# Layer 1 of a two-layer cross-attention: even entries with their image tokens first, one group of value products for two mixed tiles, M and the semantic probabilities sent with 80 rows

## The chip, the core and the metric

The kernel runs on one core of one Trainium2 chip, in one launch. The metric is device time in microseconds: the median of three runs. Beside it stands one profiled execution, from which all durations below are read.

## What is computed

Two cross-attention layers, one after the other, over 16 batch entries ("entries") of 256 query tokens with 320 channels, 20 heads of 16. The context has 256 tokens of 512 features for each entry. Layer 1 (the functions whose names end in 0) is the part that the change touches:

```python
text = encoder_hidden_states[:, :77]          # 77 text tokens
ip = encoder_hidden_states[:, 77:]            # 179 image tokens
q = hidden_states @ Wq
k_text, v_text = text @ Wk, text @ Wv
ip_k, ip_v = ip @ Wk_ip, ip @ Wv_ip
text_out = softmax(q_h k_text_h * scale) v_text_h              # for each head
text_probs = softmax((q @ k_text.T) * scale)                   # over all heads at once
q_sem = text_probs @ text
sem = (q_sem @ ip.T) * scale                                   # the same for every head
ip_probs = softmax(q_h ip_k_h * scale + 0.5 * sem) * spatial_mask
out = (text_out + ip_probs ip_v_h) @ Wout + bout + hidden_states
```

The softmax over the 77 text tokens and the one over the 179 image tokens are separate; both are taken in one tile of 256 keys. Layer 2 has the same shape with 252 text and 4 image tokens, and is unchanged.

## The kernel before

All operands are kept as a rounded high part and a low part, so a product over 512 features is a group of 12 matmuls (4 blocks of 128 features, three terms each; `prod`).

**Slots.** One slot is one group of 4 heads of one entry. Layer 1 takes slots 0 to 79 (entry b has slots 5b to 5b+4), layer 2 slots 80 to 159. Two entries, 2c and 2c+1, make a pair c and take ten slots, 10c to 10c+9. In slot k TensorE makes the scores of slot k+2 (`score0`, L737, in the PSUM tile S, of which there is one; VectorE takes their maxima, L738 text and L739 image, and so frees S), the maxima turned round (`maxima0`, L745, then an ACT copy to `mt` and four small DMAs from ACT's queue into the rows of `qs`), the transposed scores of slot k in two halves t = 0 and 1 (`turned0`, L761, PSUM tiles T), their exponentials on ACT (L764), a product with the semantic weights `rs` on GpSimd, POOL in the profile (L767), and at the next slot's first fifth the products with the values (`attend0`, `values0`, L794), 24 matmuls of 32 columns.

**Fillers.** Between these steps stand the tasks that prepare later entries. Each has a list of times in slots, and `fill` steps those that are due, so TensorE's order is fixed by these numbers; TensorE is the only engine of the main loop whose order is written, the other queues (ACT, DVE, POOL, SP) are put in order by the scheduler of the framework, each then running in its order. Tasks: `k0` (`keys0`: context of a pair loaded by `context`, split into high and low parts by `in_turn`/`halves`, L163 on ACT and L166 on POOL or DVE; then the keys), `q0` (`queries0`, with the split of x: ACT L281, POOL or DVE L282, DVE L283), `m0t` (`tokens0`: M, the products of an entry's text and image tokens), `v0` (`values0_`: the values), `s0` (`semantic0`: text probabilities turned round in `tph`; L663 on DVE reads a PSUM bank and frees it), `c0` (output product). The X banks of PSUM, three, are shared by all fillers in turn.

**Layout of an entry.** The 256 keys are text first (0 to 76), then image (77 to 255). With tiles of 128 keys, tile 0 is mixed (77 text, 51 image) and tile 1 is image alone. So `values0_` makes three groups of 12 products of 128x320 for each entry: text values of tile 0, image values of tile 0, image values of tile 1; ACT copies each to the value tile `vr` (L418), with masks `tmask` for the two of tile 0. The column of ones that gives the softmax sums is set once (`marks`). In L794 value group `vt` = 0 and 1 read P of t = 0, and `vt` = 2 reads t = 1.

**Semantic scores and maxima.** The stacks `ks` and `qs`, four of each, have 48 rows of keys or queries, from row 48 (`XROW`) 77 rows of M or of the text probabilities, and from row 125 two rows that subtract the maxima of text and of image. `stacks0` fills them by DMA from SP's queue: `ks<-kd` and `qs<-qd` (48 rows), `qs<-tph` (77 rows x 4 heads x 256) and `ks<-M` (77 x 4 x 179, the image columns alone; the text columns are zero from the start, and the two last rows of `ks` are set once by `fields`). Groups g = 0 to 3 of an entry send M and the probabilities; g = 4 finds them in its stack.

Of the kernel before, what the change touches and what calls it, by code (L numbers as in the profile page):

```python
# [26 lines left out]
T1 = S - NIP  # L27
DUP = S // 2 - NIP
# [21 lines left out]
def xattn2(  # L50
# [60 lines left out]
    words, slots = {"ctb": 1024, "cta": 1024, "raw": 512, "rawc": 512, "both": 2 * (S - T0), "kb": 936, "si": 256, "sp": 128, "wC": 2 * 4 * (H * D + NIP), "mt": S, "mx": 2, "tmp": (NG + 1) * 48, "kst": 4 * S, "rs": 2 * S, "P": 4 * S}, {}  # L111
# [77 lines left out]
    def in_turn(parts, wait, tag="raw", eng=nc.vector, later=False):  # L189

        ahead, parts, tags = [], list(parts), tag.split()
        for i in range(len(parts) + 1):
# [6 lines left out]
            for j in new:  # L199
                src, hi, lo = parts[j]  # L200
                raw = buf(tags[j // 2 % len(tags)], [128, 512], bufs=2)
                shape = src.shape
                raw = raw[:, : shape[1]] if len(shape) == 2 else raw.rearrange("p (k n) -> p k n", k=shape[1])
                (queued if later else lambda inst: inst)(dma(raw, src))
                ahead.append((hi, lo, raw))
# [55 lines left out]

    def context(b, n, wait=0):

        tiles, parts = [], []
        for k in range(0, 4, 3 - n):
            src = cT_d[:, b * S : (b + n) * S].rearrange("(k p) t -> p k t", p=128)[:, k : k + 3 - n]
            ct = buf("cta" if n == 1 or k < 2 else "ctb", [128, 2, 512], FR, bufs=SIZES["CTA" if n == 1 or k < 2 else "CTB"], name="ct")
            split = lambda t: t.rearrange("p (k t) -> p k t", t=n * S)
            parts.append((src, split(ct[:, 0]), split(ct[:, 1])))
            tiles.append(ct)  # L270
        yield from in_turn(parts, wait, "rawc raw" if b == 2 and n == 2 else "rawc", nc.gpsimd if wait and b != 2 else nc.vector, n == 2 and b > 2)
        if n == 2:
            return lambda s, k: tiles[k][:, s].rearrange("p (b t) -> p b t", b=2)
# [12 lines left out]
    ct = [buf(t, [128, 2, 512], FR, bufs=2, name="ct") for t in ("cta", "cta", "ctb", "ctb")]  # L286
    ct0 = {0: lambda s, k, tiles=ct: tiles[k][:, s].rearrange("p (b t) -> p b t", b=2)}
# [27 lines left out]
    hsn = const_tile([128, 3, 8, 2, 16], "hsn")  # L315

    def constants():
# [3 lines left out]
        for i in range(SIZES["NR"]):  # L321
            nc.gpsimd.memset(f(ks[i]), 0.0)
# [10 lines left out]

    def fields():

        ind0 = buf("nt", [128, 2, 8, 32], bufs=2, name="ind0").rearrange("p a f c -> p (a f c)")[:2, :S]
        dma(ind0, ind0_d)
        yield
        ind0r = buf("mt", [8, S], FR, name="ind0r")[:2]
        nc.scalar.copy(ind0r, ind0)  # L340
        yield
        for i in range(SIZES["NR"]):
            dma(ks[i][XROW + T0 : KS0], ind0r.unsqueeze(1).to_broadcast([2, 4, S]))
        yield
# [15 lines left out]
    def keys0(c):  # L360
# [8 lines left out]
        for m in range(3):  # L369
            kst = buf("kst", [128, 2, 2, S], FR, bufs=SIZES["KST"])  # L370
            for w, lo, hi, a, z in ((wk0, 0, T0 + 1, 0, T0), (wki0, T0 - 1, S, T0, S)):
                kp = bank()[:, : 2 * (hi - lo)].rearrange("p (b t) -> p b t", b=2)
                prod_m(kp, w, m, lambda s, k: ct(s, k)[:, :, lo:hi], 4)
                n = 64 if m == 2 else 128
                evacuate(kst[:, 0, :, a:z], kst[:, 1, :, a:z], kp[:, :, a - lo : z - lo], m)
                if a:
                    keys_out(kd[0][c], m, kst)
                else:
                    nc.gpsimd.tensor_copy(kt[:n, m, :, :, :T0], f(kst[:n, :, :, :T0]))
                yield  # L380

    def keys_first():

        ct = ct0[0]
# [27 lines left out]
    def values0_(b):  # L412
        ct, i = ct0[b // 2], b % 2
        V = vr[(b + 2) % 3]
        for t, (w,), lo, sc in ((0, wv0, 0, tmask[:, 0:1]), (1, wvi0, 0, tmask[:, 1:2]), (2, wvi0, 128, 1.0)):
            vp = bank()[:, :320]
            prod(vp, lambda s, k: ct(s, k)[:, i, lo : lo + 128], lambda s, k: w(s, k), 4)
            nc.scalar.activation(  # L418
# [979 lines left out]
```

## Time and profile before

| | |
|---|---|
| median of three runs | 1515.25 us (1510.85 to 1517.94) |
| profiled execution | 1522.64 us; span 1520.8 us, 1.84 us around it |
| mean granted TensorE clock | 0.975 |
| PE busy | 1436.6 us, 94% of the span |
| POOL, DVE, ACT busy | 1215.1, 1178.0, 884.4 us (80%, 77%, 58%) |
| DMA queue of SP and ACT | 229.44 MB, 52.7% of the 16 DMA engines |

A line of a timeline gives start and duration in us, engine, line of the kernel, operation, output <- inputs, shapes and count, and in brackets the engine's idle time before it and what ended that. SPq is SP's queue, on which the duration is that of issuing. A line of the windows gives busy time (and instructions) of PE, PEld, DVE, ACT and POOL in that stretch, then the granted clock, the mean share of the 16 DMA engines that is busy, and GB/s.

### The profile page before, as it was taken

Reading aid. Unit: us, or ns where it says so; the run is one execution under the profiler, and the core shown is the slowest. Engines: PE = TensorE matmul, PEld = TensorE weight load, DVE = VectorE, ACT = ScalarE, POOL = GpSimd, SP = SyncE. Lnnn points to the kernel's source line nnn. Section 1 sums busy time; section 2 is a strip of 40 time slices with the busy share of each in tenths; the row PEclk is TensorE's granted clock in tenths of the full one; section 3 lists DMA queues with packets and bytes.
Section 4 is the critical chain, followed back from the end, with each engine's and each line's share of the span. In section 5 each row is a group of like instructions: output and inputs, shape, how many; then the busy total and the mean of one; then the engine's idle time right before and its main releaser. Section 6 shows DMA issues by size and latency. Waiting matters only on the chain.

```text
span 1520.8 us, 36025 instructions
## 1 busy us (share of the span) xinstructions
PE 1436.6 (94%) x12726; PEld 1160.9 (76%) x12726; DVE 1178.0 (77%) x2595; ACT 884.4 (58%) x1973; POOL 1215.1 (80%) x1302
## 2 busy tenths in 40 slices
PE   8689999999999989788999999999999999999996
PEld 7678878887888778566777777777777777777764
DVE  5467777777777787867878888888888887788885
ACT  5346555655565555445665666566656666666561
POOL 4359787978888977887688789877988798879785
PEclk9899999999999999899999999999999999999997
DMA  7757766767676766665534444444444344434311
GB/s 237 208 165 216 203 192 197 214 204 209 183 213 210 210 194 172 186 198 156 147 104 120 125 124 118 130 122 114 121 134 124 107 125 131 125 108 113 103 33 37
DMA packets 228815, 233.04 MB, mean 153 GB/s; under 512 B 38410, under 2 KB 198508, under 8 KB 228620
## 3 DMA queue, kind: packets, MB, share of 16 engines
q1 hardware_dynamic: 226428, 229.44, 52.7%
q8 instruction: 102, 1.67, 0.5%
q10 hardware_dynamic: 2208, 1.30, 0.3%
q14 instruction: 77, 0.63, 0.1%
HBM read 118.04 MB, written 77.10 MB: 128 GB/s over the span
## 4 chain that ended last, share of the span: by engine, by line
PE 75%; DVE 7%; DMA 6%; issue 4%; POOL 3%; ACT 3%; SPq 1%; ACTq 0%; DVEq 0%; POOLq 0%
PE X L932 15%; PE X L238 14%; PE P L794 6%; PE X L603 5%; PE P L944 5%; PE S L737 5%; PE P L954 4%; PE T L761 4%; PE T L884 3%; PE S L890 3%; PE X L606 2%; PE X L248 2%; PE X L572 2%; DMA qs<-mt 1%; PE X L1057 1%
## 5 line engine op out<-in xcount | busy, mean ns | idle before, releaser
L767 POOL TENSOR_TENSOR P<-P,rs 128x512 f32<-128x512 f32 x320 | 415.1, 1321 | 102.5 <-ACT P L764 101.5
L923 POOL TENSOR_TENSOR wt<-P,ctb 128x512 f32<-128x512 f32 x320 | 410.3, 1307 | 78.4 <-ACT ctb L922 78.3
L932 PE MATMUL X<-ctb,gm 128*128 128x512 f32 x1120 | 305.6, 402 | 5.9 <-DVE wt L933 5.8
L764 ACT ACTIVATE P<-T 128x512 f32<-128x512 f32 x320 | 175.9, 593 | 158.6 <-PE T L761 100.0
L933 DVE TENSOR_TENSOR wt<-X,wt 128x512 f32<-128x512 f32 x320 | 216.3, 681 | 42.9 <-PE X L932 37.5
L932 PEld LDWEIGHTS X<-ctb,gm 128*128 128x128 f32 x1120 | 195.7, 189 | 39.1 <-DVE wt L933 8.5
L904 ACT ACTIVATE P<-T 128x512 f32<-128x512 f32 x320 | 173.1, 593 | 77.3 <-PE T L884 75.0
L922 ACT ACTIVATE ctb<-P 128x512 fp32r<-128x512 f32 x320 | 186.9, 627 | 38.8 <-PE X L932 35.4
L892 DVE TENSOR_REDUCE mn<-S 128x4 fp32r<-128x1008 f32 x160 | 191.4, 1196 | 0.0
L739 DVE TENSOR_REDUCE mn<-S 128x4 fp32r<-128x716 f32 x160 | 142.4, 890 | 0.0
L794 PE MATMUL P<-P,vr 128*32 128x256 f32 x1920 | 129.5, 402 | 2.2 <-DVE tmp L811 1.9
L737 PE MATMUL S<-ks,qs 125*128 125x256 f32 x640 | 117.5, 307 | 6.0 <-DVE mn L739 1.7
L737 PEld LDWEIGHTS S<-ks,qs 125*128 125x128 f32 x640 | 88.2, 194 | 41.9 <-issue 21.9
L761 PE MATMUL T<-qs,ks 127*128 127x256 f32 x640 | 108.6, 291 | 4.9 <-DMA qs<-mt 3.2
L1020 POOL TENSOR_TENSOR r<-u,rs 128x40 f32<-128x40 f32 (+2 forms) x17 | 108.7, 6395 | 3.6 <-DVE u L1017 3.6
L805 DVE STREAM_TRANSPOSE nt<-P 128x512 f32<-128x512 f32 x80 | 57.0, 713 | 56.8 <-PE P L794 56.3
L761 PEld LDWEIGHTS T<-qs,ks 127*128 127x128 f32 x640 | 91.5, 196 | 7.6 <-ACT P L764 2.1
L738 DVE TENSOR_REDUCE mn<-S 128x4 fp32r<-128x308 f32 x160 | 74.6, 466 | 28.2 <-PE S L737 27.8
L794 PEld LDWEIGHTS P<-P,vr 128*32 128x32 f32 x1920 | 57.7, 114 | 45.6 <-issue 9.5
L944 PE MATMUL P<-P,v1t 128*32 128x256 f32 x1280 | 86.3, 388 | 0.0
L954 PE MATMUL P<-wt,zone 128*32 128x256 f32 x1280 | 84.8, 379 | 0.3 <-DVE wt L933 0.3
L603 PE MATMUL X<-ho,wF 128*128 128x256 f32 x512 | 75.3, 289 | 9.2 <-ACT mt L747 4.7
(279 smaller groups left out, 2987.6 us busy)
## 6 DMA issues: line engine op xcount, KB each, us to landing
qd<-q SPq DMA_DIRECT2D x96, 256.0 KB
qs<-tph SPq DMA_DIRECT2D x64, 308.0 KB
rawc<-in_cT_dram SPq DMA_DIRECT2D x60, 256.0 KB
qs<-qd SPq DMA_DIRECT2D x80, 192.0 KB
ks<-kd SPq DMA_DIRECT2D x80, 192.0 KB
ks<-kd SPq DMA_DIRECT2D x160, 96.0 KB
qs<-qd SPq DMA_DIRECT2D x160, 96.0 KB
kd<-kst SPq DMA_DIRECT2D x57, 256.0 KB
```

What stands on the lines that cost most here:

```text
L238: last = mm(out, lhs(a, k), rhs(b, k), start=i == 0, stop=i == len(terms) - 1)
L737: mm(sp[:, h], Q[: XROW + T0, h, t * 128 : (t + 1) * 128], K[: XROW + T0, h], start=True, stop=True)
L761: mm(st[p][:, j], K[:KS0, 2 * p + j, t * 128 : (t + 1) * 128], Q[:KS0, 2 * p + j], start=True, stop=True)
L764: exp = anchor(nc.scalar.activation(pt, st[p], AF.Exp, scale=SCALE))
L767: anchor(nc.gpsimd.tensor_mul(pt, pt, rs[:, t : t + 1].to_broadcast([128, 2, S])))
L794: mm(pv[32 * s : 32 * s + 32, o : o + S], v[:, vt, h : h + 32], P[k, s // 2][:, t, s % 2], start=vt < 2, stop=vt != 1,)
L892: anchor(nc.vector.tensor_reduce(maxes[k + 2][:, t], sp[:, :, :T1], axis=AX.X, op=ALU.max))
L904: anchor(nc.scalar.activation(P[k, u][:, t], st[u], AF.Exp, scale=SCALE))
L922: nc.scalar.activation(R[k, u][:, t], P[k, u][:, t], AF.Copy, scale=0.5)
L923: anchor(nc.gpsimd.tensor_sub(W[k, u][:, t], P[k, u][:, t], f(R[k, u][:, t])))
L932: mm(yp, gm[:, gb], R[k, u][:, kt], start=i == 0, stop=i == len(blocks[n]) - 1)
L933: nc.vector.tensor_mul(W[k, u][:, n], yp, W[k, u][:, n])
```

## The change

- From pair 1 on, the context of a pair is loaded in another layout: image tokens of the even entry in columns 0 to 178, 26 spare columns, image tokens of the odd entry from 205 to 383, then the two entries' text from 384. Each load of 128 x 512 becomes two, 128 x 2 x 179 and 128 x 2 x 77. The split (ACT, POOL or DVE) then takes 538 columns instead of 512.
- Even entries from 2 on (`turned_round`) order their keys image first: tile 0 is image alone, tile 1 is mixed (51 image, 77 text). Columns 128 to 255 of the context then hold the last 51 image tokens of the even entry and the first 51 of the odd one, at the rows that their mixed tiles want, and one group of 12 products gives both; ACT copies it twice, with two masks. So from pair 1 on a pair has five groups of value products instead of six; those of the even entry are made at -7, -5.4 and -4.4 slots, those of the odd one from -3.4.
- The column of ones is set anew for each entry from 2 on (`mark`, two POOL copies of 128 x 20).
- In `values0` the even entries take t = 1 for `vt` = 0 and 1, and t = 0 for `vt` = 2.
- M and the stack of the probabilities get three more rows, set at the start, which hold the rows that choose text or image; both are sent with 80 rows and all 256 columns (M from 77 x 4 x 179, the probabilities from 77 x 4 x 256).
- `fields` no longer fills rows of `ks`, and the four memsets of `ks` at the start are gone.

```diff
+TR = T0 + 3
+LI = S - T0
+IB, TA = 205, 384
+TB, TE = TA + T0, TA + 2 * T0
+CW = TB + 128
...
+                if isinstance(src, list):
+                    raw = raw[:, :TE]
+                    if tags[j // 2 % len(tags)] == "raw":
+                        nc.vector.memset(raw[:, LI:IB], 0.0)
...
+                for to, piece in pieces:
+                    (queued if later else lambda inst: inst)(dma(to(raw), piece))
...
+    def turned_round(b):
+
+        return b > 1 and b % 2 == 0
...
+            if n == 2:
+                row = cT_d[k * 128 : (k + 1) * 128, b * S : (b + 2) * S].rearrange("p (b t) -> p b t", b=2)
+                to = lambda raw: (pair(raw, 0, IB, LI), raw[:, TA:TE].rearrange("p (b t) -> p b t", b=2))
+                src = [(lambda raw: to(raw)[0], row[:, :, T0:]), (lambda raw: to(raw)[1], row[:, :, :T0])]
...
-        for i in range(SIZES["NR"]):
-            dma(ks[i][XROW + T0 : KS0], ind0r.unsqueeze(1).to_broadcast([2, 4, S]))
+        for i in range(2):
+            fused.append(buf("M", [TR, 2, S], FR, bufs=SIZES["M"]))
+            dma(fused[i][T0:, 0], ind0r)
+            dma(buf("tph", [TR, 2, S], FR, bufs=2)[T0:, 0], ind0r)
...
-        for t, (w,), lo, sc in ((0, wv0, 0, tmask[:, 0:1]), (1, wvi0, 0, tmask[:, 1:2]), (2, wvi0, 128, 1.0)):
...
+        mixed, whole = (i * S, i * S + 128) if b < 2 else ((TA - 128 + T0, 0), (TB, S))[i]
+        mark(0, masks[0])
+        product(wv0, mixed, (V, 0, masks[0]))
+        yield
+        if b < 2:
+            product(wvi0, mixed, (V, 1, masks[1]))
+            yield
+        mark(1, masks[1])
+        product(wvi0, whole, (V, 2, 1.0))
+        yield
+        if turned_round(b):
+            product(
+                wvi0,
+                128,
+                (V, 1, masks[1]),
+                (vr[(b + 3) % 3], 1, tmask[:, 1:2]),
             )
...
+        if b == 2:
+            for to, at in ((text, slice(0, T0)), (image, slice(T0, S))):
+                dma(M[T0:, 0, to], fused[1][T0:, 0, at])
...
-                    dma(Q[XROW : XROW + T0], tph[:, 0:1].to_broadcast([T0, 4, S]))
+                    dma(Q[XROW : XROW + TR], tph[:, 0:1].to_broadcast([TR, 4, S]))
                 else:
-                    dma(K[XROW : XROW + T0, :, T0:], mh[:, 0:1, T0:].to_broadcast([T0, 4, S - T0]))
+                    dma(K[XROW : XROW + TR], mh[:, 0:1].to_broadcast([TR, 4, S]))
...
         t, o = ((0, 0), (0, S), (1, S))[vt]
+        if turned_round(k // NG):
+            t = 1 - t
...
-        task(("v0", 2 * c), shifted(n, -7, -5.4, -5), lambda b=2 * c: values0_(b), *k)
-        task(("v0", 2 * c + 1), shifted(n, -4, -3.8, -3.4), lambda b=2 * c + 1: values0_(b), *k)
+        task(("v0", 2 * c), shifted(n, -7, -5.4, -4.4), lambda b=2 * c: values0_(b), *k)
+        task(("v0", 2 * c + 1), shifted(n, -3.4, -2.4), lambda b=2 * c + 1: values0_(b), *k)
```

Three places show how the order moves. First TensorE in slot 34 and at the start of 35 (a steady pair; X are PSUM banks, wD the image value weights, cta and ctb the context, `x3` the three terms). Before:

```order
L761 MATMUL T_68<-qs2_97,ks2_101 128x256 x2
L761 MATMUL T_67<-qs2_97,ks2_101 128x256 x2
L238 MATMUL X_4263<-wD_93,cta_0_81 128x320 x3
L238 MATMUL X_4263<-wD_93,cta_1_82 128x320 x3
L238 MATMUL X_4263<-wD_94,ctb_0_83 128x320 x3
L238 MATMUL X_4263<-wD_94,ctb_1_84 128x320 x3
L238 MATMUL X_4279<-wD_93,cta_0_81 128x320 x3
L238 MATMUL X_4279<-wD_93,cta_1_82 128x320 x3
L238 MATMUL X_4279<-wD_94,ctb_0_83 128x320 x3
L238 MATMUL X_4279<-wD_94,ctb_1_84 128x320 x3
L745 MATMUL X_4297<-ident_r_79,mn_0_561 8x128 x2
L737 MATMUL S_66<-ks1_100,qs1_96 128x256 x4
```

The same place now:

```order
L841 MATMUL T_68<-qs2_97,ks2_101 128x256 x2
L841 MATMUL T_67<-qs2_97,ks2_101 128x256 x2
L250 MATMUL X_4264<-wD_93,cta_0_81 128x320 x3
L250 MATMUL X_4264<-wD_93,cta_1_82 128x320 x3
L250 MATMUL X_4264<-wD_94,ctb_0_83 128x320 x3
L250 MATMUL X_4264<-wD_94,ctb_1_84 128x320 x3
L825 MATMUL X_4284<-ident_r_79,mn_0_567 8x128 x2
L816 MATMUL S_66<-ks1_100,qs1_96 128x256 x4
```

One group of 12 products is gone here; in slot 35 the shared group takes the place of the odd entry's text values, and in slot 36 the group ahead of the value products of slot 35 has moved behind them.

Second, SP's queue at the end of the preparation before slot 0 (rawc and raw are landing buffers of the context of pair 1). Before:

```order
L83 DMA ks2_101<-M_0_280 77x4x179
L83 DMA rawc_0_117<-in_cT_dram 128x512
L83 DMA rawc_1_118<-in_cT_dram 128x512
L83 DMA raw_616<-in_cT_dram 128x512
L83 DMA raw_618<-in_cT_dram 128x512
L83 DMA kd0_70<-kst_0_158 128x2x256
```

Now:

```order
L88 DMA ks2_101<-M_0_261 80x4x256
L88 DMA rawc_0_118<-in_cT_dram 128x2x179
L88 DMA rawc_0_118<-in_cT_dram 128x2x77
L88 DMA rawc_1_119<-in_cT_dram 128x2x179
L88 DMA rawc_1_119<-in_cT_dram 128x2x77
L88 DMA raw_624<-in_cT_dram 128x2x179
L88 DMA raw_624<-in_cT_dram 128x2x77
L88 DMA raw_628<-in_cT_dram 128x2x179
L88 DMA raw_628<-in_cT_dram 128x2x77
L88 DMA kd0_70<-kst_0_164 128x2x256
```

Four issues have become eight, ahead of everything that SP sends for the first slots.

Third, POOL in slot 35 (P are the probabilities, hsn the gathered output, hq the split of x). Before:

```order
L812 TENSOR_TENSOR hsn_109<-tmp_1_803 128x8x16
L767 TENSOR_TENSOR P_2_122<-P_2_122,rs_1_115 128x512
L767 TENSOR_TENSOR P_3_123<-P_3_123,rs_1_115 128x512
L767 TENSOR_TENSOR P_2_122<-P_2_122,rs_1_115 128x512
L767 TENSOR_TENSOR P_3_123<-P_3_123,rs_1_115 128x512
L282 TENSOR_TENSOR hq_0_229<-xq_0_91,hq_0_229 128x512
```

Now:

```order
L894 TENSOR_TENSOR hsn_109<-tmp_1_815 128x8x16
L505 MEMSET M_1_262 77x2x77
L847 TENSOR_TENSOR P_2_123<-P_2_123,rs_1_116 128x512
L471 COPY vr_103<-tmask_80 128x20
L847 TENSOR_TENSOR P_3_124<-P_3_124,rs_1_116 128x512
L471 COPY vr_103<-tmask_80 128x20
L847 TENSOR_TENSOR P_2_123<-P_2_123,rs_1_116 128x512
L847 TENSOR_TENSOR P_3_124<-P_3_124,rs_1_116 128x512
L313 TENSOR_TENSOR hq_0_235<-xq_0_91,hq_0_235 128x512
```

The two copies of the column of ones stand between the products of the slot's first half, and the memset of M (in the row before it stood after a later slot's work) ahead of them.

123 lines of the change are left out of this document (78 added, 45 removed).

## The prediction

> **What bounds the kernel now.** I read the page first, then the windows of five pairs of layer 1, then TensorE's list of waits, then timelines of single slots. The page's row of busy times:
>
> ```profile
> PE 1436.6 (94%) x12726; PEld 1160.9 (76%) x12726; DVE 1178.0 (77%) x2595; ACT 884.4 (58%) x1973; POOL 1215.1 (80%) x1302
> ```
>
> An average over two layers, so I cut layer 1 at the starts of the transposed scores that begin pairs (slots 10c). The five windows, each one pair long (start:end, length, busy of PE, PEld, DVE, ACT, POOL, clock, DMA share, GB/s):
>
> ```profile
> 302.30:381.10 78.80, 75.27 (x703) 64.58 (x702) 60.92 (x139) 44.31 (x106) 65.86 (x64) 0.98 0.71 208
> 381.10:456.90 75.80, 74.17 (x703) 63.90 (x702) 57.93 (x138) 44.36 (x105) 65.77 (x64) 1.00 0.69 201
> 456.90:536.90 80.00, 75.71 (x702) 64.93 (x702) 60.85 (x143) 44.52 (x105) 68.26 (x67) 0.98 0.71 210
> 227.20:302.30 75.10, 74.03 (x702) 63.76 (x701) 57.53 (x136) 43.98 (x105) 65.64 (x64) 1.00 0.68 202
> 146.20:227.20 81.00, 76.78 (x703) 65.64 (x702) 60.54 (x136) 44.18 (x104) 65.13 (x63) 0.96 0.68 198
> ```
>
> Two kinds stand here. The clean pairs take 75.10 and 75.80 us at clock 1.00 with PE busy for 98%: there TensorE's own work is the time. The others take 78.80, 80.00 and 81.00 with the same instructions; the mean difference is 79.93 - 75.45 = 4.48 us. TensorE's waits between 100 and 700 us (total, times, longest) say what differs:
>
> ```profile
> PE X L238 <- DVE sp L663: 6.5, 3, 2.5
> ...
> PE T L761 <- DMA qs<-mt: 1.9, 3, 1.0
> ...
> PE S L737 <- DVE mn L739: 0.3, 1, 0.3
> ```
>
> Three waits of up to 2.5 us for a PSUM bank that `sp` (L663 on DVE) reads, one in each slower pair. Waits for DMA and for the maxima are small. So a steady pair is bound by PE, with a stall in about every second one.
>
> **The change part by part.**
>
> *The products that go.* Four rows of slot 34 (start, duration) measure a group of 12:
>
> ```profile
> 335.47 1.04 PE L238 MATMUL X<-wD,cta 128*128 128x320 f32 x6
> 336.36 1.04 PE L238 MATMUL X<-wD,ctb 128*128 128x320 f32 x6
> 337.24 1.04 PE L238 MATMUL X<-wD,cta 128*128 128x320 f32 x6
> ...
> 339.00 0.28 PE L745 MATMUL X<-ident_r,mn 128*8 128x128 f32 x2
> ```
>
> The third group begins 337.24 - 335.47 = 1.77 us after the first, so 12 products cost 1.77 us (the durations overlap in the pipeline). One group goes from each of seven pairs: 7 x 1.77 = 12.4 us. No wait ends there, and the work is on the path. But it is worth its full price only where PE is the bound. The window at layer 1's end, where the output products and layer 2's preparation stand, is another case:
>
> ```profile
> 600.00:700.00 100.00, 83.08 (x764) 64.94 (x763) 79.95 (x173) 51.89 (x119) 84.38 (x91) 0.93 0.65 185
> ```
>
> PE is busy for 83%, POOL for 84 and DVE for 80. The values of the last pair lie ahead of this, its slots in it, so I give half of the last 1.77 back: +0.9, between 0 and 1.8.
>
> *Image first, t = 1 first.* In even entries 16 of the 24 value matmuls now want P of t = 1, which POOL finishes last; before, only the last 8 did. Slot 33 is the tight case:
>
> ```profile
> 330.58 2.54 POOL L767 TENSOR_TENSOR P<-P,rs 128x512 f32<-128x512 f32 x2 [0.98 <-ACT P L764]
> 332.99 1.50 PE L794 MATMUL P<-P,vr 128*32 128x256 f32 x24
> ```
>
> POOL ends at 330.58 + 2.54 = 333.12, PE starts the 24 at 332.99. Now it must wait some 0.2 us (0.13 and the signal). In the other slots of an entry POOL is done earlier. It cannot gain, as t = 0 is always the earlier half. One slot in a pair: 7 x 0.2 = +1.4; if none is tight 0, if three of five are 4.2.
>
> *The marks.* Four more POOL copies of 128 x 20 in a pair. The trace has no such copy; the nearest small POOL instructions are these (busy in all, mean ns), with two rows on POOL's room:
>
> ```profile
> L814 POOL COPY hsn<-hsn 128x128 f32<-128x128 f32 x8 | 2.3, 293 | 0.0
> L428 POOL MEMSET M<- 77x154 f32 x8 | 1.8, 227 | 4.8 <-PE X L689 4.7
> 341.25 2.52 POOL L767 TENSOR_TENSOR P<-P,rs 128x512 f32<-128x512 f32 x2 [2.12 <-ACT P L764]
> 344.50:365.90 21.40, 21.17 (x200) 18.28 (x202) 16.56 (x36) 13.77 (x29) 21.37 (x21) 1.00 0.70 201
> ```
>
> Each costs 0.23 to 0.29 us, so about 1.0 in a pair; POOL's gap of 2.12 before 341.25 hides two of them, and I cost all at 0. Where POOL is dense, as in 344.5 to 365.9 (21.37 of 21.40 busy), there is no cover: 28 x 0.26 = 7.3 us would be the most. A copy only adds to POOL, so nothing is gained. I take 0, since PE is as dense there as POOL and moves by its own work.
>
> *Wider splits.* 538 columns instead of 512 are 5% more. POOL's 128 x 512 subtraction takes 1.29 us (row at 370.84 below), so +0.07, and ACT's 0.62 (row at 52.06) gives +0.03; ACT is busy for 44 of 75 us in a pair. Hidden: 0.
>
> *Start.* SP issues eight loads instead of four ahead of the first slots:
>
> ```profile
> 46.86 1.65 SPq L83 DMA_DIRECT2D rawc<-in_cT_dram  x2
> 48.55 0.91 SPq L83 DMA_DIRECT2D raw<-in_cT_dram  x2
> 49.50 2.49 SPq L83 DMA_DIRECT2D kd<-kst  x4
> 389.90 1.72 SPq L83 DMA_DIRECT2D qd<-q  x3
> 52.06 0.62 ACT L163 CAST cta<-rawc 128x512 fp32r<-128x512 f32 x1 [3.72 <-DMA rawc<-in_cT_dram]
> 55.66 0.28 PE L745 MATMUL X<-ident_r,mn 128*8 128x128 f32 x1 [5.14 <-DMA kd<-kst]
> 58.05 0.87 SPq L83 DMA_DIRECT2D ks<-M  x1
> 62.85 1.20 PE L737 MATMUL S<-ks,qs 125*128 125x256 f32 x4 [1.64 <-DMA ks<-M]
> ```
>
> SP issues without a gap here, and PE waits: 5.14 us before 55.66, 1.64 before 62.85 for `ks<-M`, which SP issued at 58.05. A load with 256 runs costs 1.72 / 3 = 0.57 to issue, eight 4.6; the four took 1.65 + 0.91 = 2.56. So `kd<-kst` and what follows slide by up to +2.0. At best the loads hide and the 1.64 goes too: -1.6. I take +1.5, since every row behind them waits in one queue, and what is first wanted still starts at 46.86. The four small constants that are added and the four that go balance, and `ks` loses four memsets that nobody waited for.
>
> *80 rows x 256 for M and the probabilities.* `ks<-M` carries 80 x 256 for 77 x 179, 49% more, `qs<-tph` 4% more. In the steady pairs PE never waits for either. A window in which only 77-row transfers fly:
>
> ```profile
> 332.20:332.90 0.70, 0.70 (x8) 0.66 (x6) 0.70 (x2) 0.29 (x1) 0.70 (x1) 1.00 0.71 211
> ```
>
> DMA share 0.71, about 11 engines of 16. The Trainium skill, "DMA: Bandwidth & Descriptors", section "Why a DMA increments its semaphore by 16 and not by 1", says that a transfer is dealt to the largest number of engines up to 16 that divides its partitions: by that 77 rows use 11 and 80 use all 16, and the window agrees. By it alone the wait of 1.64 at 62.85 would go and the sum would be 1505.0. I keep 0: the main loop has at most 1.9 us of waits for DMA to win, and 49% more bytes stand against it.
>
> *The sum.* -12.4 + 0.9 + 1.4 + 1.5 = -8.6. On the profiled execution 1522.64 - 8.6 = 1514.0. That execution lies 7.4 us above the median of 1515.25; the difference cannot be seen in one trace, and I take the change off the median: **1506.6 us**.
>
> **The rivals.** They all turn on one stall. The row for slot 39 and its like:
>
> ```profile
> 368.36 2.55 POOL L767 TENSOR_TENSOR P<-P,rs 128x512 f32<-128x512 f32 x2
> 370.84 1.29 POOL L282 TENSOR_TENSOR hq<-xq,hq 128x512 fp32r<-128x512 f32 x1
> 372.06 0.48 POOL L812 TENSOR_TENSOR hsn<-tmp 128x128 f32<-128x128 f32 x1
> ...
> 369.38 3.45 DVE L283 SCALAR_TENSOR_TENSOR hq<-hq,tmask,xq 128x256 fp32r<-128x256 f32 x1
> 372.75 0.22 DVE L663 TENSOR_TENSOR sp<-sp,X 128x77 f32<-128x77 f32 x1
> 373.03 1.27 PE L238 MATMUL X<-cta,wB 128*128 128x360 f32 x6 [2.48 <-DVE sp L663]
> ...
> 295.08 0.48 DVE L283 SCALAR_TENSOR_TENSOR hq<-hq,tmask,xq 128x256 fp32r<-128x256 f32 x1 [0.50 <-ACT hq L281]
> 374.20:377.60 3.40, 3.40 (x23) 2.21 (x25) 1.24 (x5) 1.48 (x5) 2.31 (x2) 0.50 0.60 150
> ```
>
> DVE's part of the split of x (L283) takes 0.48 us in a clean pair (295.08) and 3.45 at 369.38, as long as POOL runs without a gap (368.36 to 372.5). Behind it waits `sp` (372.75), which holds a PSUM bank, and PE idles 2.48 us; then it runs at half clock for 3.4 us. The Trainium skill, "SBUF — State Buffer", section "SBUF: two separate sides", calls the ports shared by VectorE and GpSimd an exclusive lock for one whole instruction. By that the wait would end with one POOL instruction, 1.3 us; here it lasted through three, so the measurement decides. Whether the stall comes depends on which of the two engines starts first, tenths of a us, and every edit above moves that.
>
> - *A, the sum:* three stalls as before. 1506.6, by its bounds and the spread of the runs 1500 to 1513.
> - *B, fewer stalls:* PE with less work asks for POOL's and DVE's results at other times, and two of three stalls go. 1506.6 - 2 x 4.48 = 1497.6. For it: there are three to lose, and each hangs on tenths of a us; against it: nothing in the change aims at them.
> - *C, POOL and DVE set the pace:* POOL is busy for 65.7 of 75.8 us and gets 1.2 more (marks, splits); its dense stretch of 21.4 us is no longer covered by PE, and PE's shorter work turns into waits for P. Then the 12.4 is given back whole: 1515.25 + 1.5 + 1.4 = 1518.2. Against it: outside that stretch POOL has 2 us gaps.
> - *D, the other side, stalls in more pairs:* the marks lengthen POOL's runs at the head of a slot, where L283 then starts behind them. Each further pair costs 4.48. Two cancel the gain (1515.6); with four more, all seven stalling, 1506.6 + 17.9 = 1524.5. It decides from the third on. For it: three of five pairs do it already; against it: two clean pairs with the same rows.
> - That the products do not go is excluded by the order, where 28 rows of three are gone: 84 matmuls.
>
> **How the numbers follow.** A change of 0.5%, 7.6 us, is about what a measurement of this kernel can tell from none: faster is below 1507.7, slower above 1522.8. A has 0.40, as the only case whose terms are all in rows; its centre lies just below the edge, so 0.22 faster and 0.18 same. B has 0.18, all faster. C 0.20, all same. D 0.22, of it 0.17 slower and 0.05 same. Faster 0.40, same 0.43, slower 0.17. The range goes from 1496, which takes in B's centre, to 1523, which takes in A, C and the near half of D; it leaves out about 0.2. Faster and same hold most of the chance; the likeliest case alone spans 1500 to 1513.
>
> **What would show it.** In the profile after: the wD and wC groups of a pair shorter by 12 products and clean pairs near 74 us (right) or still 75 to 76 (C); one wait of TensorE's value matmuls for POOL's P of about 0.2 us in a pair, not more; the number of pairs with 2.5 us of idle time before a wB product behind `sp` (three: A; none or one: B; five or more: D); the wait for `ks<-M` at the start shorter or gone, and slot 0 later by about 1.5. A median above 1522.8 would make the forecast wrong, and so would one near 1515 with clean pairs at 74, because the loss would then be in a place that I have not costed.

## The result, and the profile after

The changed kernel takes 1528.89 us (median of seven runs, 1523.07 to 1536.06), the kernel before 1510.85 us (median of seven, 1509.45 to 1517.94, the first three among them): a ratio of 1.0111, 95% interval 1.0086 to 1.0136. It is slower by 18.0 us between the medians, about 17 us by the ratio, where 8.6 us less were forecast. The profiled execution after took 1533.67 us with a span of 1531.7.

The page of after, its busy times:

```profile
PE 1431.7 (93%) x12642; PEld 1151.7 (75%) x12642; DVE 1190.9 (78%) x2597; ACT 885.2 (58%) x1973; POOL 1217.0 (79%) x1334
```

TensorE has its 84 matmuls less, and DVE, which was given almost nothing to do, is busy for 12.9 us more. The windows of five pairs of after, columns as before (start:end, length, busy PE, PEld, DVE, ACT, POOL, clock, DMA share, GB/s):

```profile
155.40:231.00 75.60, 72.43 (x691) 62.24 (x690) 59.42 (x137) 44.64 (x104) 66.74 (x68) 1.00 0.84 229
231.00:307.10 76.10, 72.50 (x691) 62.10 (x690) 59.16 (x137) 44.55 (x104) 66.60 (x68) 1.00 0.81 219
307.10:383.50 76.40, 72.90 (x691) 62.23 (x690) 61.96 (x137) 44.80 (x104) 66.35 (x68) 1.00 0.82 216
...
459.90:537.80 77.90, 73.31 (x690) 62.66 (x690) 61.42 (x142) 44.33 (x104) 68.61 (x70) 0.99 0.78 209
```

A clean pair should have become 74 us long. PE's busy time did fall, from 74.0 to 72.5 us, but the pair takes 75.6 to 76.4, as long as before or longer: 3 to 4 us of idle time stand where 1 to 1.6 us stood. The DMA share rose from about 0.69 to about 0.82. So the clean pairs lost what the products gave. But the pairs are not where the changed kernel falls behind. The starts of the transposed scores divide three profiles, of one execution each (us; the second profile of the kernel before is taken up below):

| | ahead of slot 10 | slots 10 to 59 | slots 60 to 78 | from slot 79 on |
|---|---|---|---|---|
| before, the profile of the prediction | 146.2 | 390.7 | 161.3 | 822.6 |
| before, second profile | 147.4 | 383.6 | 159.6 | 823.4 |
| after | 155.4 | 382.3 | 167.6 | 826.3 |

In slots 10 to 59 the kernel before has stalls that the changed one has not, and the changed one is not slower there. It is longer than both ahead of slot 10 (by 8 to 9 us), in slots 60 to 78 (6 to 8) and behind them (3 to 4). TensorE's waits of after, between 100 and 700 us:

```profile
PE X L757 <- ACT sp L753: 6.3, 2, 5.6
PE X L738 <- DVE q L272: 4.8, 6, 1.8
...
PE X L825 <- DVE kst L171: 2.8, 5, 1.3
...
PE X L250 <- DVE sp L741: 2.6, 1, 2.6
PE X L825 <- ACT q L168: 2.4, 5, 0.5
...
PE S L816 <- DMA qs<-tph: 1.4, 1, 1.4
...
PE P L876 <- POOL P L847: 0.3, 1, 0.3
```

Many waits of about half a microsecond, once in most pairs, have come up: for banks that DVE and ACT free and for transfers. The waits of a wB product for `sp`, three of which would have been the sign of A and none or one that of B, are down to one (L250, in slot 9): the stalls did become fewer, and the time rose all the same. The largest wait, 5.6 us in slot 69, was 4.0 before.

Two of the places in which much is lost at once lie outside the steady pairs. At the start: SP's queue and TensorE's wait for `ks<-M` in after, and the window of slot 1 of before and then of after:

```profile
45.72 4.08 SPq L88 DMA_DIRECT2D rawc<-in_cT_dram  x4
49.91 1.95 SPq L88 DMA_DIRECT2D raw<-in_cT_dram  x4
...
64.67 1.19 PE L816 MATMUL S<-ks,qs 125*128 125x256 f32 x4 [2.43 <-DMA ks<-M]
```

```profile
63.80:77.90 14.10, 12.97 (x100) 11.85 (x99) 6.02 (x13) 4.71 (x11) 7.71 (x8) 0.89 0.69 189
```

```profile
65.70:83.30 17.60, 16.10 (x99) 13.92 (x99) 6.09 (x13) 4.82 (x12) 9.73 (x10) 0.71 0.59 167
```

The eight loads take 4.08 + 1.95 = 6.03 us of SP, not 4.6; the wait grows from 1.64 to 2.43, and slot 1 is 3.5 us longer at clock 0.71 instead of 0.89. Of these 3.5 us 3.1 are busy time of PE, and busy time times clock is the same in both (11.5 and 11.4 us): it is the same work at a lower clock. Slot 1 is no steady measure, though. It took 15.94 us in the second profile of the kernel before, and 17.75 in one of the kernels below that has no cut loads (80 rows and a pause). And early in layer 2, where the program is unchanged, DVE's and POOL's timeline with TensorE's row behind it:

```profile
789.31 0.47 POOL L1105 TENSOR_TENSOR a<-tmp,r 128x160 f32<-128x160 f32 x1
...
789.52 4.93 DVE L314 SCALAR_TENSOR_TENSOR hq<-hq,tmask,xq 128x256 fp32r<-128x256 f32 x1
...
789.73 0.21 POOL L1078 COPY tmp<-nt 128x48 f32<-128x48 f32 x1
789.91 1.30 POOL L313 TENSOR_TENSOR hq<-xq,hq 128x512 fp32r<-128x512 f32 x1
...
791.18 0.52 POOL L1107 TENSOR_TENSOR a<-a,si 128x160 f32<-128x160 f32 x1
...
791.67 2.50 POOL L1005 TENSOR_TENSOR wt<-P,ctb 128x512 f32<-128x512 f32 x2
...
796.09 0.80 PE L972 MATMUL S<-ks,qs 48*128 48x256 f32 x4 [3.35 <-DVE wt L1015]
```

It is the stall of rival D at another place: DVE's piece of the split (0.48 us when free) lasts 4.93 us, to just behind the end of POOL's run at 794.17, and TensorE idles 3.35. But few pieces that meet POOL are held for a whole run. Of the line's 64 pieces in both layers, 36 took under 0.75 us in the kernel before, 25 between 0.75 and 2, and 3 longer; in the changed one 27, 33 and 4. Here is one of the 25, in the kernel before, with POOL's rows around it:

```profile
524.02 2.95 POOL L767 TENSOR_TENSOR P<-P,rs 128x512 f32<-128x512 f32 x2 [1.03 <-ACT P L764]
...
525.90 1.34 DVE L283 SCALAR_TENSOR_TENSOR hq<-hq,tmask,xq 128x256 fp32r<-128x256 f32 x1
...
526.93 1.47 POOL L282 TENSOR_TENSOR hq<-xq,hq 128x512 fp32r<-128x512 f32 x1
...
528.48 0.45 POOL L812 TENSOR_TENSOR hsn<-tmp 128x128 f32<-128x128 f32 x1
```

It ends at 527.24, 0.27 us behind the end of POOL's pair (524.02 + 2.95 = 526.97), while POOL's next instruction runs to 528.40: it waited for the instruction in progress and got through ahead of the rest. What decides between one instruction and a whole run is not shown here. Summed over layer 1 and the opening of layer 2 (groups by line, 56 to 830 us: total us, mean ns), this line of before (L283) and of after (L314):

```profile
L283 DVE SCALAR_TENSOR_TENSOR ho<-ho,tmask,hT 128x256 fp32r<-128x256 f32 x17 | 20.2, 1188 | 0.0
L283 DVE SCALAR_TENSOR_TENSOR hq<-hq,tmask,xq 128x256 fp32r<-128x256 f32 x18 | 17.3, 963 | 0.8 <-ACT hq L281 0.7
```

```profile
L314 DVE SCALAR_TENSOR_TENSOR ho<-ho,tmask,hT 128x256 fp32r<-128x256 f32 x17 | 26.3, 1547 | 0.0
L314 DVE SCALAR_TENSOR_TENSOR hq<-hq,tmask,xq 128x256 fp32r<-128x256 f32 x18 | 21.7, 1206 | 1.4 <-ACT hq L312 1.2
```

The same 35 pieces took 37.5 us before and 48.0 after, one long one more and more waits for one instruction.

### The profile page after: what moved, and what is told of

It is laid out like the page before. It is cut to its first block, busy times and chain, and to the rows that moved or that the text cites. A ratio compares the mean times of both kernels' runs of the same rounds, so it can differ in the third digit from the quotient of the medians.

```text
span 1531.7 us, 35974 instructions
## 1 busy us (share of the span) xinstructions
PE 1431.7 (93%) x12642; PEld 1151.7 (75%) x12642; DVE 1190.9 (78%) x2597; ACT 885.2 (58%) x1973; POOL 1217.0 (79%) x1334
## 4 chain that ended last, share of the span: by engine, by line
PE 70%; DMA 9%; DVE 8%; POOL 4%; issue 3%; ACT 3%; SPq 2%; ACTq 1%; DVEq 0%; POOLq 0%
PE X L1014 15%; PE X L250 12%; PE P L876 6%; PE X L681 6%; PE P L1026 5%; PE S L816 4%; PE P L1036 4%; PE S L972 3%; PE T L966 3%; PE T L841 3%; SPq L88 2%; PE X L260 2%; PE X L684 2%; PE X L650 2%; PE X L1139 1%
## 5 line engine op out<-in xcount | busy, mean ns | idle before, releaser
L818 DVE TENSOR_REDUCE mn<-S 128x4 fp32r<-128x308 f32 x160 | 74.9, 468 | 37.5 <-PE S L816 36.9
```

## The experiments

All ratios are against the kernel before, run on the same chip; its medians there lay between 1512.6 and 1514.7 us.

**One part at a time, in the kernel before.** First the products: in even entries from 2 on, the text values are copied into both masked groups.

```diff
+            less = b > 1 and b % 2 == 0
+            if less and t == 1:
+                yield
+                continue
             vp = bank()[:, :320]
...
-            nc.scalar.activation(
+            for u in (0, 1) if less and t == 0 else (t,):
+                nc.scalar.activation(
```

> The kernel before, and in each even entry from 2 on the second group of 12 value products is left out (the text values are copied twice instead, so those image values are wrong): 84 matmuls less, and nothing else of the change. Theory 1 (TensorE's own work is the time, as the prediction had it; the loss lies in the rest of the change): 8 to 13 us faster than before. Theory 2 (the removed group covered the latency of other engines, whose pace sets the time once it is gone): within 4 us of before, with new idle time of TensorE in the slots where the group stood. Either way the profile says how long a clean pair is: 73.5 us by the first, 75 or more by the second.

Measured: 1517.98 us, ratio 1.0022 (0.9994 to 1.0050). Leaving out the 84 matmuls wins nothing; the interval leaves at most 1 us. The two pairs without a long stall took 74.2 and 74.8 us, between the two theories. Theory 2 holds as to the time; why is taken up below.

Second, the loads cut in two:

```diff
-                (queued if later else lambda inst: inst)(dma(raw, src))
+                cut = [(raw, src)]
+                if later or len(tags) > 1:
+                    two = lambda a: a[:, 0].rearrange("p (b t) -> p b t", b=2)
+                    cut = [(two(raw)[:, :, s], two(src)[:, :, s]) for s in (slice(T0, S), slice(0, T0))]
+                for to, piece in cut:
+                    (queued if later else lambda inst: inst)(dma(to, piece))
```

> The kernel before, with each context load from pair 1 on issued as two (128 x 2 x 179 and 128 x 2 x 77) into the old places: nothing else of the change. Theory 1 (SP's issues and the short runs are where the change loses): 8 us or more slower than before, at least 4 of it before slot 10. Theory 2 (they are hidden but for the start): 1 to 3 us slower, all of it in slots 0 to 3.

Measured: 1531.74 us, ratio 1.0107 (1.0071 to 1.0144). By itself this part loses as much as the whole change. Theory 1 holds in the total; its "at least 4 before slot 10" does not in the one profile, where slots 0 and 1 were 3.6 us longer and slot 4 shorter by 4.1.

Third, the 80 rows (with the three rows of constants set at the start, as in the change):

```diff
-                    dma(Q[XROW : XROW + T0], tph[:, 0:1].to_broadcast([T0, 4, S]))
+                    dma(Q[XROW : XROW + TR], tph[:, 0:1].to_broadcast([TR, 4, S]))
...
-                    dma(K[XROW : XROW + T0, :, T0:], mh[:, 0:1, T0:].to_broadcast([T0, 4, S - T0]))
+                    dma(K[XROW : XROW + TR], mh[:, 0:1].to_broadcast([TR, 4, S]))
```

> The kernel before, with M and the probabilities sent with 80 rows and 256 columns: nothing else of the change. If the 49% more bytes of M cost (theory 1): 4 us or more slower, waits for DMA in the slots 5 to 9 of a pair and a DMA share near 0.8. If 16 transfer engines for 11 and the shorter issue (0.65 us for 0.90 in the profile after) make up for it (theory 2): within 3 us of before, or faster.

Measured: 1509.39 us, ratio 0.9955 (0.9932 to 0.9977): faster, as theory 2 allowed, and the best complete kernel of this study. Its pair from slot 20 to 29, and the issue of `ks<-M` that took 0.87 us in before:

```profile
217.40:292.30 74.90, 73.83 (x702) 63.78 (x701) 57.72 (x136) 43.92 (x104) 65.53 (x64) 1.00 0.82 222
```

```profile
56.78 0.66 SPq L84 DMA_DIRECT2D ks<-M  x1
```

DMA is busier, 0.82, the issue shorter, and PE as busy as in a clean pair of before.

**Parts taken out of the changed kernel.** The context loaded in one piece, with the layout made by the split:

```diff
-                src = [(lambda raw: to(raw)[0], row[:, :, T0:]), (lambda raw: to(raw)[1], row[:, :, :T0])]
-                parts.append((src, ct[:, 0, :TE], ct[:, 1, :TE]))
+                parts.append((row, [
+                    (pair(ct[:, 0], 0, IB, LI), pair(ct[:, 1], 0, IB, LI), lambda raw: two(raw)[:, :, T0:]),
+                    (two(ct[:, 0, TA:TE]), two(ct[:, 1, TA:TE]), lambda raw: two(raw)[:, :, :T0]),
+                ], None))
```

> The changed kernel with each context load from pair 1 on as one transfer of 128 x 512 again; the new layout is made by the split instead (ACT and POOL or DVE each take two pieces, image and text, for one). If the cut loads are where the change loses (theory 1, after the kernel before with cut loads came out 1.1% slower): 10 to 20 us faster than the changed kernel, so within 8 us of the kernel before. If it is the new order of work that loses (theory 2): within 5 us of the changed kernel.

Measured: 1533.83 us, ratio 1.0126 (1.0079 to 1.0172). Theory 1 falls in this form, and the time is that of theory 2: whole loads save nothing if ACT and POOL or DVE then make 28 splits in two pieces each. Whether these splits cost what the whole loads save, or another part of the change costs as much with whole loads, this run does not tell.

The 77 rows put back (the two `dma` lines above reversed; `fields` fills the two last rows of `ks` once, with the constant -0.5):

> The changed kernel with M and the probabilities sent with 77 rows again (77 x 4 x 179 and 77 x 4 x 256) and the two rows that choose text or image set once with the value -0.5 (so the keys of the turned entries get wrong semantic rows and maxima). After the gain of 0.45% with 80 rows in the kernel before, 4 to 10 us slower than the changed kernel (theory 1); if the cut loads have used up the DMA engines' room, no difference or a gain (theory 2).

Measured: 1532.21 us, ratio 1.0106 (1.0067 to 1.0145), the same as the changed kernel. Theory 2 as to the time: what 80 rows gained in the kernel before does not show there. That the cut loads have used up the room, as the theory had it, is not shown.

Only pair 1 cut in two, in the kernel before (`if len(tags) > 1`):

> The kernel before with the loads of pair 1 alone cut in two, the four that stand in SP's queue ahead of the first slots. If the loss of the cut loads lies at the start (theory 1): 8 us or more slower than before. If it lies in the steady pairs (theory 2): 2 to 5 us slower, the 3.6 us that slots 0 and 1 were longer in the profile with all loads cut.

Measured: 1516.70 us, ratio 1.0013 (0.9988 to 1.0038). Its profile has slots 0 and 1 longer by 1.45 and 3.05 us, but the median is only 2 us higher. Theory 2: most of the cut loads' loss comes from the later loads.

**The line that POOL holds up.** First its work was moved:

```diff
-        order(nc.vector.scalar_tensor_tensor(hl[:, 2], f(hl[:, 2]), neg, src[:, 2], op0=ALU.mult, op1=ALU.add))
+        if tag == "hq":
+            order(nc.gpsimd.tensor_sub(hl[64:, 2], src[64:, 2], f(hl[64:, 2])))
+        else:
+            order(nc.vector.scalar_tensor_tensor(hl[:, 2], f(hl[:, 2]), neg, src[:, 2], op0=ALU.mult, op1=ALU.add))
```

> The kernel before with the third piece of x's split (L283 on DVE for layer 1, 128 x 256) replaced by a subtraction of its lower 64 partitions on POOL. If the stalls of 4 to 6 us come from DVE waiting behind POOL's run at this line (theory 1): 4 to 12 us faster, the waits for sp gone, fewer slots with an excess over 2 us, and a smaller spread of the runs. If POOL's own time is the bound there (theory 2): same or slower, with TensorE waiting for P of POOL instead.

Measured: 1561.89 us, ratio 1.0310 (1.0263 to 1.0357): much slower, but not with the waits for P of theory 2. TensorE waits for the maxima, and the timeline of slot 17 shows theory 1's mechanism at another line (DVE, POOL, then TensorE):

```profile
PE S L740 <- DVE mn L742: 22.2, 6, 4.5
```

```profile
205.76 6.06 DVE L282 TENSOR_TENSOR ho<-hT,ho 128x512 fp32r<-128x512 f32 x1 [1.36 <-ACT ho L281]
205.89 1.29 POOL L166 TENSOR_TENSOR cta<-rawc,cta 128x512 fp32r<-128x512 f32 x1
207.14 0.46 POOL L815 TENSOR_TENSOR hsn<-tmp 128x128 f32<-128x128 f32 x1
207.56 1.27 POOL L166 TENSOR_TENSOR cta<-rawc,cta 128x512 fp32r<-128x512 f32 x1
208.79 2.48 POOL L770 TENSOR_TENSOR P<-P,rs 128x512 f32<-128x512 f32 x2
213.47 1.22 PE L740 MATMUL S<-ks,qs 125*128 125x256 f32 x4 [4.25 <-DVE mn L742]
```

The other piece of the gathered output's split, 0.67 us when free, lasts 6.06, until POOL's five instructions have ended (208.79 + 2.48 = 211.27). The maxima are queued behind it, and TensorE waits 4.25. Six of the 32 pieces of this line took 4.9 to 6.3 us, where the longest had taken 1.81 in the kernel before: with POOL's new order another line is held. So the next three kernels leave the line out altogether (the same line deleted in the kernel before, in the changed one and in that with cut loads):

> The kernel before without the third piece of the splits of x and of the gathered output (L283 on DVE, 128 x 256, for hq and ho; the low part of channels 256 to 319 is then wrong). Its own work is 33 x 0.48 us on DVE, off TensorE's path. If the stalls that TensorE suffers come from this line held behind POOL's runs (theory 1): 5 to 12 us faster than before. If another operation takes its place as the one held (theory 2, as L282 did when this piece went to POOL): within 3 us of before.

> The changed kernel without the same line. Theory 1: the change is slower because more of these are held behind POOL (31.7 us of excess at this line in the profile after, 20.8 in that of before), so without it the distance to the kernel before without it falls from 1.1% to under 0.5%. Theory 2: the distance stays above 0.8%, and the loss is in other waits (PSUM banks that ACT and DVE free, transfers).

> The kernel before with all context loads from pair 1 on cut in two, without the same line. Theory 1: the 1.1% of the cut loads fall under 0.4% against the kernel before without the line. Theory 2: they stay above 0.8%, and cutting the loads costs by itself, through later landings.

Measured: 1493.81 us, ratio 0.9867 (0.9841 to 0.9893); 1502.69 us, 0.9938 (0.9917 to 0.9960); 1502.53 us, 0.9936 (0.9913 to 0.9960). Leaving out DVE's pieces of 0.48 us is worth 1.3% in the kernel before, 1.7% in the other two: theory 1 of the first, well beyond its 12 us. The long stalls alone do not make this: between a third and a half of it, 11.5 of 30.5 us against the first profile of the kernel before and 12.2 of 23.7 against the second, lies behind the start of slot 79, where none of its pieces takes 2 us. The distance of the changed kernel shrinks from 1.1 to 0.7%, that of the cut loads the same: between the theories. About a third of the loss goes with this line; with intervals of 0.3% on each side, that share is not sharp.

The kernel before once more, for its stalls:

> The kernel before, unchanged, for a second profile: which of its stalls over 2 us (slots 4, 19, 39, 59, 64 in the first) come again. If they hang on tenths of a microsecond, they stand in other slots and are fewer, since the first profiled run was 7 to 12 us above the median.

Measured: 1515.83 us. Of the three waits of L238 for `sp` one is left, in slot 59. There `sp` waits behind a product of 64 x 512 on DVE, which lasts 3.73 us beside a run of POOL and took 1.05 in the first profile. The waits and the timeline:

```profile
PE X L238 <- DVE sp L663: 2.9, 1, 2.9
```

```profile
517.06 3.73 DVE L449 TENSOR_TENSOR rawc<-rawc 64x512 f32<-64x512 f32 x1 [0.30 <-issue]
```

So the stalls change from run to run, and the profiled run on which the prediction stood, with three of them, was 12 us above the median of seven.

Last, a complete kernel, 80 rows and a pause in POOL's run (`third` is DVE's piece, now issued ahead of `rest`, POOL's, which waits for it):

```diff
+        if eng is nc.gpsimd:
+            tc.add_manual_dep(rest.ins, third.ins.name, mybir.DependencyInfo(mybir.DependencyClass.Sync, mybir.DependencyReason.DATA), reason="port")
```

> A complete kernel: the kernel before with 80 rows, and POOL's part of x's split (128 x 512) made to wait for DVE's part of it, so that POOL's run has a pause in which DVE gets through. If DVE is held until POOL pauses (theory 1): the long ones among the 128 x 256 pieces of hq fall under 2.5 us, and the time 2 to 8 us under that of 80 rows alone (ratio under 0.994). If the wait costs POOL as much as it saves (theory 2): within 2 us of 80 rows alone, 0.994 to 0.997, or slower.

Measured: 1515.42 us, ratio 1.0020 (0.9999 to 1.0040). The longest pieces of `hq` without and with the pause:

```profile
359.55 3.37 DVE L284 SCALAR_TENSOR_TENSOR hq<-hq,tmask,xq 128x256 fp32r<-128x256 f32 x1 [0.22 <-ACT hq L282]
```

```profile
518.76 1.34 DVE L283 SCALAR_TENSOR_TENSOR hq<-hq,tmask,xq 128x256 fp32r<-128x256 f32 x1
```

The long piece is gone, as theory 1 had it, but it is one piece, and the second profile of the kernel before has none of `hq` over 1.62 us without a pause. No time is won (theory 2): against 80 rows alone 0.65% are lost. One wait of 2.5 us for `sp` is still there, and DVE's larger piece of `ho`, now behind the other, took 51.7 us in its 32 instructions instead of 35.3. Whether that is the loss is not shown.

**Where the 12 products' time goes.** Without the line, again with fewer products, with 80 rows, and with both:

> The kernel before with the group of 12 products left out in even entries from 2 on, and without the third piece of the splits (L283): to be set against the kernel before without that piece (1493.8 us, 0.9867 of before). The term of the prediction was 7 x 1.77 = 12.4 us; with L283 in place the same edit gained nothing. If the stalls behind POOL had eaten it (theory 1): 8 to 12 us faster than the kernel without the piece, ratio to before under 0.981. If the saved time is given back in the same pair to the next wait, for the transfers of the stacks and for banks that ACT and DVE free (theory 2): within 4 us of it, ratio 0.984 to 0.990.

> The kernel before with 80 rows and 256 columns for M and the probabilities, and without L283: to be set against the kernel before without it (0.9867). If the 0.45% that 80 rows gained came from fewer stalls at L283 by luck of the phase (theory 1): within 2 us of it, ratio 0.985 to 0.988. If it comes from transfers that land sooner (theory 2): 4 to 8 us faster than it, ratio 0.981 to 0.984.

> The kernel before with the group of 12 left out in even entries from 2 on, with 80 rows for M and the probabilities, and without L283; to be set against the same with all products (0.9848, 1488.1 us). In the profile of the fewer products alone the next slot waited for the stack's transfer qs<-qd, 4.8 us in four waits. If the transfers of that slot are what takes the saving back and 80 rows make them land sooner (theory 1): 5 to 10 us faster than with all products, ratio 0.978 to 0.982. If the bound there is not eased by 80 rows (theory 2): within 3 us of it, ratio 0.983 to 0.987, and the wait in the slot after the group is still there.

Measured: 1491.78 us, ratio 0.9871 (0.9843 to 0.9899); 1488.07 us, 0.9848 (0.9820 to 0.9875); 1494.59 us, 0.9864 (0.9837 to 0.9892). The ratios side by side:

| | all work | without L283 |
|---|---|---|
| before | 1 | 0.9867 |
| fewer products | 1.0022 | 0.9871 |
| loads cut in two | 1.0107 | 0.9936 |
| 80 rows | 0.9955 | 0.9848 |
| fewer products, 80 rows | not run | 0.9864 |
| the change | 1.0111 | 0.9938 |

Against 0.9867, and with 80 rows against 0.9848, the fewer products gain nothing that can be measured, although the stalls of L283 cannot hide it: theory 2 in both. With intervals of 0.3% on each side the forecast 12.4 us (0.8%) are excluded, 4 us are not. The profile of the first shows where the time goes. TensorE's largest sum of waits there, in slots 5, 15, 35 and 45, of which the kernel that makes all products has 0.3:

```profile
PE S L741 <- DMA qs<-qd: 4.8, 4, 2.6
```

SP's queue and TensorE at slot 45, and the window between issue and wait; then the same of the kernel that makes all products.

```profile
400.23 1.51 SPq L83 DMA_DIRECT2D xq<-in_xT_dram  x1
...
402.71 0.52 SPq L83 DMA_DIRECT2D qs<-qd  x1
...
409.55 0.71 PE L741 MATMUL S<-ks,qs 125*128 125x256 f32 x4 [2.58 <-DMA qs<-qd]
```

```profile
402.70:409.50 6.80, 4.27 (x44) 3.44 (x36) 3.46 (x8) 2.93 (x7) 6.12 (x6) 1.00 0.92 222
```

```profile
401.09 0.43 SPq L83 DMA_DIRECT2D xq<-in_xT_dram  x1
...
402.50 0.52 SPq L83 DMA_DIRECT2D qs<-qd  x1
...
408.67 0.69 PE L736 MATMUL S<-ks,qs 125*128 125x256 f32 x4
```

```profile
402.50:408.60 6.10, 6.10 (x64) 5.17 (x64) 4.33 (x9) 3.59 (x8) 3.87 (x4) 1.00 0.94 261
```

SP issues `qs<-qd` at 402.7 and 402.5, no earlier for TensorE's being ahead; here the issue of `xq` ahead of it took 1.51 us for 0.43. In the five pairs from 10 to 59 it is issued 7.1 to 8.2 us behind the start of the slot with the group when the products are fewer, and 6.9 to 7.9 with all. With all products TensorE is at the scores at 408.67 and does not wait; with fewer it is there at 406.97 (409.55 - 2.58) and waits until 409.5. The DMA engines are busy for 0.92 to 0.94 between. Slot 44 became 1.8 us shorter, slot 45 1.9 longer, the most of the five. Together the slots 14, 24, 34, 44 and 54 gave 8.3 us (1.8, 1.7, 1.4, 1.8, 1.6); 4.8 came back in the slots right behind them (0.4, 0.6, 1.3, 1.9, 0.6), most of the rest in slots 19 and 59 (1.7 and 1.8), and 0.9 were left at slot 60. This execution, 1484.88 us, is the fastest of its six; a lead of 6.3 us that it has in slots 60 to 69 does not show in the medians.

The changed kernel has the same wait in some pairs. The windows of slot 25 in before and after, and TensorE in after:

```profile
264.60:271.50 6.90, 6.89 (x71) 5.78 (x69) 5.14 (x11) 4.20 (x9) 4.64 (x4) 1.00 0.83 237
```

```profile
267.40:275.80 8.40, 6.97 (x70) 5.92 (x69) 5.16 (x11) 4.67 (x12) 7.02 (x9) 1.00 0.81 220
...
275.26 0.72 PE L816 MATMUL S<-ks,qs 125*128 125x256 f32 x4 [1.43 <-DMA qs<-tph]
```

Slot 24 is 1.57 us shorter and slot 25 1.45 longer; slot 35 is 1.43 longer, with a wait of 1.24 for `qs<-mt`. Slots 15, 45 and 55 do not show it.

For 80 rows without L283 (0.9848 against 0.9867) the two intervals overlap: whether their gain lives in the transfers or in the phase of the stalls stays open.

## Why the prediction was wrong, point by point

- **The products, -12.4.** The step that failed is "there TensorE's own work is the time", read from 98% busy. The count was right, 84 matmuls, and slot 34 is shorter by 1.57 us. But alone the edit measured +0.2%, and without L283 +0.04% against the kernel without it. 98% says who is busy, not how close the next bound is: in the slot behind, the transfers for the stacks held nobody up, but a TensorE that came to slot 45's scores 1.7 us sooner found them not yet landed. The clean pairs of 75.6 to 76.4 us are the sign of rival C. What took more than half of the saving back in the slot behind was another engine than C named, DMA for POOL.
- **The loads, "hidden" in the steady pairs and +1.5 at the start.** This is the largest error: cutting them costs 1.07%, about 16 us, by itself. The start costs 1.3 and 3.6 us in slots 0 and 1 of after, above the upper bound of 2.0, because the price per issue came from another transfer (0.57; the eight took 0.75) and the longer wait was followed by a slot at clock 0.71. Cutting the loads of pair 1 alone moved the median by 2 us, so most of the price belongs to the later loads, for which the prediction worked out no term at all. Where it is paid, single profiles do not agree: with the loads alone cut, slots 10 to 59 took 396.1 us against 390.7 and 383.6 in the two of the kernel before; in the changed kernel they took 382.3, and the loss stood ahead of them and behind.
- **80 rows, 0.** Taken alone they gain 0.45%. The Trainium skill, "DMA: Bandwidth & Descriptors", section "Why a DMA increments its semaphore by 16 and not by 1", stood against the zero. The rows do not contradict it: the share was 0.71 where only 77-row transfers flew, and the mean of a pair went from about 0.70 to 0.82 with 80 rows; a stretch with 80-row transfers alone is not shown. The 1.64 us at the start that the rule would have removed did not go: 2.04 with 80 rows alone, 2.43 in after. Bytes and rows together were a gain, but the changed kernel had no use for it (1.0106 without, 1.0111 with).
- **t = 1 first, +1.4.** Measured 0.3 us in one wait for POOL's P between 100 and 700 us; the marks and the 538 columns do not show as waits of their own. The sum of the three parts alone, 0.22 + 1.07 - 0.45 = 0.84%, leaves 0.3% for these and the new order, within the intervals; no run has these parts alone.
- **Rival D.** The stall of a DVE piece behind a whole run of POOL is real, and the place was too narrow: it came at L283 in slots 9, at other lines (the product in slot 59, the larger piece of `ho` with POOL's new order) and in layer 2. But it is rare, 3 of 64 pieces in the kernel before and 4 in the changed one, and the changed kernel had one wait for `sp` where three had stood, so D did not come as it was described. The whole line, its own work and its short waits included, costs the kernel before about 19 us and the changed one 26, which carries about a third of the loss; the 0.7% that remain without the line are as much as the cut loads cost without it. The stalls were priced from a profile with three of them as if that were the usual run; the second profile has one.

What stays open: why cut loads cost 0.7% without L283. In the profiles slots 0 and 1 explain 4.5 us of 9; for the others there are half-microsecond differences in slots 8, 9 and 0 of a pair and one of 5.3 us in slot 59, seen and not isolated. Open as well is why whole loads in the new layout did not win the price of the cut ones back.

## What to carry to other kernels

An engine that is 98% busy is the bound only until its work shrinks: before pricing a saving, look for the wait that comes next and how early it can come, here a transfer that was issued at about the same time with or without the saving. Work on a queue whose transfer engines are busy for 0.7 of the time is not hidden because nobody waits for it in the profile. Where stalls differ from run to run, take several profiles before pricing one, and ask of every edit whether it moves the two engines that collide.

## What the runs showed of the hardware

- A DVE operation with two SBUF inputs, 0.48 or 0.67 us when free, sometimes lasted until POOL's run of instructions without a gap had ended: 3.45, 4.93 and 6.06 us, through as many as five whole POOL instructions; the last had started 0.13 us ahead of POOL's first. Of the 64 pieces of L283, though, 36 took under 0.75 us and 25 between 0.75 and 2, like the 1.34 us at 525.90, which ended 0.27 us behind the POOL instruction in progress and 1.16 ahead of the end of the next. The Trainium skill, "SBUF — State Buffer", section "SBUF: two separate sides", gives the lock for one instruction; waits like the last agree with it, and the long ones show that DVE did not always get in between two instructions of POOL.
- A transfer of 80 rows was issued in 0.66 us where one of 77 rows with fewer bytes took 0.87, and the DMA engines' mean busy share rose from about 0.70 to 0.82 in the pairs while the kernel became faster.
